# An attention mixture whose code is written out for half tiles of 64 tokens instead of whole tiles of 128

## The chip, the cores and the metric

The kernel runs on one core of a Trainium2 chip, in one launch. The metric is the device time of that launch in microseconds (us); smaller is better. Seven runs of the kernel before gave a median of 4628.34 us (4620.35 to 4635.69).

## The reference, cut to what matters

Four sequences of 1024 tokens with 256 channels go through four layers, each added to its input after a layer norm: a causal attention, a mixture of four attention experts, a second causal attention, and a mixture of 64 small feed-forward experts. The change touches the second layer alone:

```python
logits = x @ router_w + router_b
probs = jax.nn.softmax(logits, axis=-1)
_, top2 = jax.lax.top_k(probs, 2)
for e in range(e_total):                       # 4 experts
    member = (top2 == e).any(-1)
    w_tok = jnp.where(member, probs[..., e], 0.0)
    order = jnp.argsort((~member).astype(jnp.int32), axis=-1, stable=True)
    xg = jnp.take_along_axis(x, order[..., None], axis=1)   # members first
    ...
    q = (xg @ wq[e] + bq[e]).reshape(b, s, h, hd)           # 16 heads of 16
    k, v = ...
    att = jnp.einsum('bqhd,bkhd->bhqk', q, k) * sm_scale
    att = jnp.where(validg[:, None, None, :], att, -1000000000.0)
    att = jax.nn.softmax(att, axis=-1)
    y = jnp.einsum('bhqk,bkhd->bqhd', att, v).reshape(b, s, d)
    y = y @ wo[e] + bo[e]
    out = out.at[bidx, order].add(wg[..., None] * y)
```

Every token belongs to two experts. In each expert a sequence's members attend to each other without a causal mask; tokens that are no members get weight 0, so their rows need not be computed.

Evaluating the reference's first layer and its router on the given inputs gives these numbers of members:

| | expert 0 | expert 1 | expert 2 | expert 3 |
|---|---|---|---|---|
| sequence 0 | 707 | 204 | 346 | 791 |
| sequence 1 | 749 | 189 | 323 | 787 |
| sequence 2 | 705 | 240 | 305 | 798 |
| sequence 3 | 700 | 201 | 333 | 814 |
| largest | 749 | 240 | 346 | 814 |
| tiles of 128 for the largest | 6 | 2 | 3 | 7 |
| half tiles of 64 for the largest | 12 | 4 | 6 | 13 |

## The kernel before

**Routing.** While the first attention runs, `route0` computes each token's rank among the experts, copies the rows of the members of each expert together into an array `xc` in device memory, and counts the tiles that each expert and sequence needs: `more` compares the count with 0, 128, 256, ... (`self.tiles`), and the sum of the comparisons goes into `n_of`.

**The choice of code.** `layer0_ffn` takes for each expert the largest number over the four sequences, loads it into a register and jumps into one of `NT + 1` = 9 copies of the expert's code (`tc.Switch`), written out for 0 to 8 tiles. All four sequences run in the chosen copy, each as one job of `run_attention`. `expert0` builds a job: `prepare` loads and transposes the `n` tiles of rows and makes `kc` (the key mask), `make_qk` projects queries (`pq`, `qa`) and keys (`pk`, `ka`) for a group of four heads, `values` projects the values, and `finish` applies the output matrix.

**Units and steps.** A job has four groups of heads (`g`), and its queries are cut into one half for up to four tiles, or into two (`units_of`): seven tiles become halves of 512 and 384 tokens. A pair of group and half is a unit. Softmax needs each query's largest score first, so a unit has two kinds of step:

- max steps: for one query tile of 128 (`q`), one half of the keys and one pair of heads, two matmuls of 32 contraction rows (L294), whose weights are the 128 queries and whose moving operand is the half's keys; VectorE reduces them to maxima (L309);
- exp steps: for one key tile and one pair of heads, two matmuls (L329) whose weights are 128 keys and whose moving operand is the unit's queries; ScalarE takes the exponential (L340). The negated maximum has been added into a spare row of the queries before (`set_max`: a reduction L365, a transpose of each query tile L372, an addition L376).

`times_v` (L394) multiplies the exponentials with the values: per call four matmuls with weights of 128 rows and 32 columns, each over half of the unit's queries. `divide` copies the sums (L408), transposes them (L412) and divides by the sum of exponentials (L416, L417).

**The order.** `_run_attention` writes TensorE's, VectorE's and ScalarE's orders out by hand in ticks. A tick issues one max step of a unit ahead, one exp step of a unit behind, and one call of `times_v` for exponentials two or three ticks old. `next_max` chooses, of the max steps left in a unit, one that uses the other pair of heads than the tick's exp step and whose width is nearest to it. The four heads of a group lie in rows 0 to 31, 32 to 63, 64 to 95 and 96 to 127, so a tick's four matmuls of L294 and L329 use four different quarters of TensorE's rows.

**Buffers.** PSUM has two score tiles for max steps (`s1`, two banks each), three one-bank tiles for exp steps, transposed maxima and transposed sums (tag `t`), and one bank for the sums `av`.

All matrices are 32-bit floats, and each such matmul appears in the trace as two passes with a weight load each, except for transposes, which take one.

Of the kernel before, what the change touches and what calls it, by code (L numbers as in the profile page):

```python
# [10 lines left out]
F32 = mybir.dt.float32  # L11
# [4 lines left out]
AF = mybir.ActivationFunctionType  # L16
# [5 lines left out]
P = 128  # L22
# [22 lines left out]
class Kernel:  # L45
# [121 lines left out]
        self.n_v += 1  # L167
        return self.v_buf[self.n_v % 2]

    def project(self, w, g, xnT, name, n=NT):  # L170

        nc = self.nc
        pt = self.ps.tile([P, 2, 512], F32, tag="s", name=name)
        for h in range((n + 3) // 4):
            wd = min(512, n * P - h * 512)
            for c in range(2):
                nc.tensor.matmul(  # L177
                    pt[:, h, 0:wd],
                    lhsT=w[:, c, g * P : (g + 1) * P],
                    rhs=xnT[:, c, h * 512 : h * 512 + wd],  # L180
                    start=(c == 0),
                    stop=(c == 1),
                )
        return pt.rearrange("p h t -> p (h t)")[:, 0 : n * P]

    def project_v(self, w, xnT, v, n=NT):
        nc = self.nc
# [44 lines left out]
    def units_of(self, job, causal):  # L232

        n = job["n"]
        first = n if n <= 4 else (n + 1) // 2
        halves = [(0, first * P)] + ([(first * P, (n - first) * P)] if n > first else [])
        units = []
        for g in range(NG):
            for k, (at, w) in enumerate(halves):
                nq = w // P  # L240
                u = dict(job=job, g=g, k=k, q0=at, nq=nq, es={}, last=k == len(halves) - 1)

                parts = halves[: k + 1] if causal else halves
                u["n_half"] = len(parts)
                u["max"] = [
                    (q, half, pair) for q in range(nq) for half in range(len(parts)) for pair in range(2)
                ]
                u["halves"] = parts
                n_kt = (at + w) // P if causal else n

                u["kts"] = [n_kt - 1, n_kt - 2, *range(n_kt - 2)] if causal else list(range(n_kt))
                u["exp"] = [(kt, pair) for kt in u["kts"] for pair in (1, 0)]
                units.append(u)
        return units
# [10 lines left out]
    def next_max(self, u, b, causal):  # L265


        left = u["left"]
        if b is None:
            return left.pop(0)  # L270
        o, (kt, pair) = b
        width = o["nq"] * P - self.exp_from(o, kt, causal)
        best = min(
            left, key=lambda s: (s[2] == pair, abs(self.max_width(u, s, causal) - width))
        )
        left.remove(best)
        return best

    def both(self, a, b, causal, c=None):
# [5 lines left out]
        if a is not None:  # L285
            u, (q, half, pair) = a
            qa, ka = u["qk"]
            q0 = u["q0"] + q * P
            k0 = u["halves"][half][0]
            w = self.max_width(u, (q, half, pair), causal)  # L290
            s = self.ps.tile([P, 2, 512], F32, tag="s", name="s1")
            for jj in range(2):
                r = 32 * (2 * pair + jj)
                nc.tensor.matmul(  # L294
                    s[:, jj, 0:w],
                    lhsT=qa[r : r + 32, q0 : q0 + P],
                    rhs=ka[r : r + 32, k0 : k0 + w],
                    start=True,
                    stop=True,
                )  # L300
            mx = u["mx"][:, q, 2 * pair : 2 * pair + 2, half]

            def maxima(s=s, w=w, diag=causal and half == u["k"]):
                if diag:
                    d = s[:, :, w - P : w]
                    nc.vector.tensor_tensor(  # L306
                        d, d, self.mask.unsqueeze(1).to_broadcast([P, 2, P]), ALU.add
                    )
                nc.vector.tensor_reduce(mx, s[:, :, 0:w], AX.X, ALU.max)  # L309

            reduce.append(maxima)
        for part in (b, c):
# [3 lines left out]
            qa, ka = u["qk"]  # L316
            q0 = self.exp_from(u, kt, causal)
            diag = causal and kt * P >= u["q0"]
            end = u["nq"] * P
            e = self.pp.tile([P, 2, 512], F32, tag="e", name="e")  # L320
            u["es"].setdefault(kt, {})[pair] = e, q0
            both = self.ps.tile([P, 2, 512], F32, tag="s", name="s3") if part is c else None
# [33 lines left out]
                )  # L356
        return reduce, exps

    def set_max(self, u):

        nc = self.nc
        nq = u["nq"]
        self.n_mx += 1
        m = self.mx_buf[self.n_mx % 2]
        nc.vector.tensor_reduce(  # L365
            m[:, 0:nq, :, ROW_MAX], u["mx"][:, 0:nq, :, 0 : u["n_half"]], AX.X, ALU.max, negate=True
        )
        yield
        yield
        pm = self.ps_m.tile([P, 512], F32, tag="t", name="pm")  # L370
        for q in range(nq):
            nc.tensor.transpose(  # L372
                pm[:, q * P : (q + 1) * P], m[:, q].rearrange("p h r -> p (h r)"), self.ident
            )
        part = u["qk"][0][:, u["q0"] : u["q0"] + nq * P]
        nc.vector.tensor_tensor(part, pm[:, 0 : nq * P], part, ALU.add)  # L376
        yield

    def times_v(self, u, kt, half):

        nc = self.nc
        first = kt == u["kts"][0]
        if first and half == 0:
            u["av"] = self.ps_av.tile([P, 512], F32, tag="av", name="av")
        pairs = u["es"][kt] if half == 0 else u["es"].pop(kt)
        v = u["job"]["v"]
        end = u["nq"] * P
        for j in range(4):
            e, q0 = pairs[j // 2]
            mid = (q0 + end) // 2  # L390
            c0, c1 = (q0, mid) if half == 0 else (mid, end)
            c = (4 * u["g"] + j) * VW

            nc.tensor.matmul(  # L394
                u["av"][32 * j : 32 * j + 32, c0:c1],
                lhsT=v[:, kt, c : c + 32],
                rhs=e[:, j % 2, c0 - q0 : c1 - q0],
                start=(first and half == 0),
                stop=(kt == u["kts"][-1]),
                skip_group_check=True,  # L400
            )

    def divide(self, u):
# [1 line left out]
        nc = self.nc  # L405
        g, nq, i0 = u["g"], u["nq"], u["q0"] // P
        avs = self.p2.tile([P, 512], F32, tag="avs", name="avs")
        nc.scalar.copy(avs[:, 0 : nq * P], u["av"][:, 0 : nq * P])  # L408
        yield
        pt = self.ps_m.tile([P, 4, 4, 32], F32, tag="t", name="py")  # L410
        for q in range(nq):
            nc.tensor.transpose(  # L412
                pt[:, q].rearrange("p h r -> p (h r)"), avs[:, q * P : (q + 1) * P], self.ident
            )
        rec = self.p2.tile([P, 4, 4], F32, tag="rec", name="rec")
        nc.vector.reciprocal(rec[:, 0:nq], pt[:, 0:nq, :, HD])  # L416
        nc.vector.tensor_tensor(  # L417
            u["job"]["y"][:, i0 : i0 + nq, 64 * g : 64 * (g + 1)].rearrange(
                "p q (h d) -> p q h d", d=HD
            ),  # L420
            pt[:, 0:nq, :, 0:HD],
            rec[:, 0:nq].unsqueeze(3).to_broadcast([P, nq, 4, HD]),
            ALU.mult,
        )
        yield

    def project_out(self, y, wo, give, n=NT):
# [257 lines left out]
    def ffn_constants(self):  # L685
# [21 lines left out]
        for b in range(B):  # L707
# [11 lines left out]
            self.base, pattern=[[T, E0]], base=0, channel_multiplier=0,  # L719
            allow_small_or_imprecise_dtypes=True,  # L720
        )
        self.tiles = rp.tile([1, NT], F32, tag="tiles", name="tiles")
        nc.gpsimd.iota(
            self.tiles, pattern=[[P, NT]], base=0, channel_multiplier=0,
            allow_small_or_imprecise_dtypes=True,
        )
        self.place = fp.tile([P, T], U16, tag="place", name="place")
# [4 lines left out]
    def route0(self, b):  # L732
# [38 lines left out]
        for i in range(NT):  # L771
# [16 lines left out]
        )  # L788
        cnt = rp.tile([P, E0], F32, tag=f"cnt{b}", name="cnt")
        nc.vector.tensor_copy(cnt, pc[:, nb : nb + E0])  # L790
        more = sm.tile([1, E0, NT], F32, tag="more", name="more")
        nc.vector.tensor_tensor(
            more, cnt[0:1, :].unsqueeze(2).to_broadcast([1, E0, NT]),
            self.tiles.unsqueeze(1).to_broadcast([1, E0, NT]), ALU.is_gt,
        )
        nc.vector.tensor_reduce(self.n_of[:, b, :], more, AX.X, ALU.add)
        at = sm.tile([P, NT, E0], F32, tag="at", name="at")
# [66 lines left out]
    def layer0_ffn(self):  # L864
# [18 lines left out]
        for e in range(E0):  # L883

            ahead = self.new_rows()
            for r in range(0, NT, 2):
# [6 lines left out]
            bias = self.out_bias(self.f1, f"bias{e % 2}", ins["f_bv"][e], ins["f_bo"][e], w["o"])  # L893
            following = load(e + 1) if e + 1 < E0 else None
            count = nc.values_load(
                n_tiles[0:1, e : e + 1], min_val=0, max_val=NT,
                skip_runtime_bounds_check_because="a sum of NT comparisons",
            )
            for n in tc.Switch(count, NT + 1):

                jobs = [self.expert0(b, e, n, w, bias, None if b else ahead) for b in range(B)]
                if e == E0 - 1:
# [7 lines left out]
                            pass  # L910
            w = following

    def expert0(self, b, e, n, w, bias, rows):

        nc = self.nc
        cnt = self.routed[b]["cnt"]

        def prepare(job, rows=rows):
# [34 lines left out]
        def make_qk(job, g):  # L953
            qa = self.qk.tile([P, T], F32, tag="qa", name="qa")
            ka = self.qk.tile([P, T], F32, tag="ka", name="ka")
            job["qk", g] = qa, ka
            pq = self.project(w["q"], g, job["xnT"], "pq", n)
            nc.scalar.activation(  # L958
                qa[:, 0 : n * P], pq, AF.Identity, bias=self.f_bq[:, e, g : g + 1], scale=0.5
            )  # L960
            yield
            pk = self.project(w["k"], g, job["xnT"], "pk", n)
            nc.vector.scalar_tensor_tensor(  # L963
                ka[:, 0 : n * P], pk, self.f_bk[:, e, g : g + 1], job["kc"][:, 0 : n * P],
                ALU.add, ALU.add
# [3 lines left out]
        def give(i, m, po):  # L969
# [7 lines left out]
            )  # L977

        return dict(
            n=n, prepare=prepare, make_qk=make_qk, values=values,  # L980
            finish=lambda job: self.project_out(job["y"], w["o"], give, n),
        )

# [629 lines left out]
```

## Time and profile before

| | |
|---|---|
| median of 7 runs | 4628.34 us |
| the profiled execution's own time | 4634.12 us |
| its span, from the first to the last instruction | 4632.4 us |
| mean granted clock of TensorE | 0.952 |
| TensorE busy with matmuls | 4357.2 us, 94% of the span |
| VectorE busy | 2634.6 us, 57% |
| ScalarE busy | 1909.8 us, 41% |
| GpSimd busy | 626.8 us, 14% |
| expert 0's stage (768 tokens) | about 971 to 1730 us |
| experts 1 and 2 (256 and 384 tokens) | about 1730 to 2167 us |
| expert 3's stage (896 tokens) | about 2168 to 3121 us |

Lines marked L and a number are lines of the kernel. A line of the table of groups names line, engine, operation, the tiles out<-in and their shapes; for matmuls "32*128 32x384" is a stationary operand of 32 rows and 128 columns and a moving operand of 384 columns. PE is TensorE's matmuls, PEld its weight loads, DVE VectorE, ACT ScalarE, POOL GpSimd. Matmul ends are modelled, and a matmul's duration holds the time in which it drains, which the next one can overlap; the distance between starts is what a sequence costs.

### The profile page before, as it was taken

How to read it: one execution, taken by the hardware profiler on the slowest of the kernel's cores; microseconds unless marked ns; L12 is line 12 of the kernel's file. 1: busy time of each engine (PE TensorE's matmuls, PEld its weight loads, DVE VectorE, ACT ScalarE, POOL GpSimd, SP SyncE). 2: the span in 40 equal slices, each digit the busy share in tenths (PEclk: the TensorE clock that was granted, in tenths of full speed). 3: DMA queues.
4: the chain of work that ended last, by engine and by line, in shares of the span. 5: the costliest groups of instructions: out<-in, count | busy, mean ns of one | idle time of the engine just before them, and what ended most of it. 6: DMA issues, size and time to landing. Idle time of an engine off the chain costs nothing. (4 is left out here: it accounts for less than half of the span.)

```text
span 4632.4 us, 88434 instructions
## 1 busy us (share of the span) xinstructions
PE 4357.2 (94%) x38042; PEld 2056.9 (44%) x38042; DVE 2634.6 (57%) x4505; ACT 1909.8 (41%) x4087; POOL 626.8 (14%) x671
## 2 busy tenths in 40 slices
PE   7999999979999999898999999997999899998898
PEld 3444445444444445444343444443444444443556
DVE  5766666646556544453666666655767566474232
ACT  1444444525555553343454555451343333233331
POOL 1002020110000000000001010102111423415243
PEclk8999999979999999999999999998999899897999
DMA  6004000010000000000000000001000111102586
GB/s 217 2 1 134 9 20 4 29 39 8 8 8 8 8 30 25 22 26 26 1 9 27 14 27 1 27 10 32 6 1 28 65 37 49 58 29 88 140 188 170
DMA packets 134455, 188.93 MB, mean 41 GB/s; under 512 B 14816, under 2 KB 116448, under 8 KB 133216
## 3 DMA queue, kind: packets, MB, share of 16 engines
q1 hardware_dynamic: 91584, 99.11, 6.8%
q0 software_dynamic: 27264, 66.18, 5.1%
q10 hardware_dynamic: 15136, 17.20, 1.2%
q8 instruction: 314, 5.14, 0.5%
q14 instruction: 157, 1.29, 0.1%
HBM read 83.36 MB, written 99.09 MB: 39 GB/s over the span
## 5 line engine op out<-in xcount | busy, mean ns | idle before, releaser
L340 ACT ACTIVATE e<-s 128x512 f32<-128x512 f32 (+3 forms) x3428 | 1545.9, 499 | 1855.9 <-PE s L329 1067.8
L309 DVE TENSOR_REDUCE mx<-s 128x2 f32<-128x1024 f32 (+3 forms) x1760 | 1725.0, 981 | 757.0 <-PE s L329 604.3
L329 PE MATMUL s<-qa,ka 32*128 32x384 f32 (+3 forms) x7040 | 1884.7, 558 | 57.0 <-ACT e L340 27.6
L294 PE MATMUL s<-ka,qa 32*128 32x384 f32 (+3 forms) x7040 | 1711.1, 565 | 66.9 <-DVE mx L309 24.7
L394 PE MATMUL av<-e,v 128*32 128x256 f32 (+3 forms) x14080 | 951.0, 346 | 22.8 <-ACT e L346 9.1
L294 PEld LDWEIGHTS s<-ka,qa 32*128 32x128 f32 x7040 | 551.9, 190 | 672.7 <-issue 405.7
L329 PEld LDWEIGHTS s<-qa,ka 32*128 32x128 f32 x7040 | 722.3, 188 | 135.8 <-ACT e L340 64.1
L394 PEld LDWEIGHTS av<-e,v 128*32 128x32 f32 x14080 | 298.8, 111 | 793.8 <-issue 712.3
L306 DVE TENSOR_TENSOR s<-s,mask 128x256 f32<-128x256 f32 x512 | 218.8, 427 | 244.5 <-PE s L294 175.8
L975 POOL DMA_DIRECT2D xc<-os x24 | 18.1, 754 | 2008.1 <-DVE os L971 2008.1
L1270 POOL DMA_INDIRECT xs<-rowsx,dest x192 | 184.8, 963 | 223.1 <-DVE dest L1269 157.0
L353 PEld LDWEIGHTS <-ident_b 128*32 128x32 bf16 x4096 | 62.8, 96 | 245.7 <-issue 232.2
L353 PE MATMUL s<-mask_kq,ident_b 128*32 128x128 bf16 x4096 | 154.8, 232 | 0.0
L177 PE MATMUL pq<-xT,wq 128*128 128x512 f32 (+2 forms) x384 | 148.0, 524 | 2.0 <-ACT xT L942 2.0
L93 POOL TENSOR_SCALAR rows<-x,rstd,shift 128x256 f32<-128x256 f32 x96 | 51.8, 554 | 724.8 <-DVE shift L82 714.8
L445 PE MATMUL po<-wo,yT 128*128 128x256 f32 x544 | 129.5, 390 | 11.5 <-ACT yT L440 11.5
L177 PE MATMUL pk<-xT,wk 128*128 128x512 f32 (+2 forms) x384 | 139.1, 499 | 0.1
L963 DVE SCALAR_TENSOR_TENSOR ka<-pk,bk,kc 128x768 f32<-128x768 f32 (+3 forms) x64 | 52.3, 818 | 151.8 <-PE pk L177 151.8
L1441 POOL DMA_INDIRECT sum<-ye,idx x64 | 99.9, 1561 | 159.5 <-DVE ye L1439 90.5
L376 DVE TENSOR_TENSOR qa<-pm,qa 128x512 f32<-128x512 f32 (+2 forms) x160 | 97.1, 607 | 40.0 <-PE pm L372 37.4
L958 ACT ACTIVATE qa<-pq,bq 128x768 f32<-128x768 f32 (+3 forms) x64 | 47.4, 740 | 173.4 <-PE pq L177 173.4
L445 PEld LDWEIGHTS po<-wo,yT 128*128 128x128 f32 x544 | 101.1, 192 | 36.9 <-ACT yT L440 17.2
(205 smaller groups left out, 3274.5 us busy)
## 6 DMA issues: line engine op xcount, KB each, us to landing
xc<-empty SPq DMA_DIRECT2D x4, 4096.0 KB
gu<-in_e_gu SPq DMA_DIRECT2D x64, 256.0 KB
xs<-empty ACTq DMA_DIRECT2D x16, 642.0 KB
xg<-xs SPq DMA_DIRECT2D x64, 160.5 KB
dn<-in_e_dn SPq DMA_DIRECT2D x64, 128.0 KB
sum<-sum SPq DMA_DIRECT2D x12, 512.0 KB
rows<-xc SPq DMA_DIRECT2D x19, 256.0 KB
xc<-os POOLq DMA_DIRECT2D x8, 512.0 KB
```

The lines of the kernel that those rows point to most:

```text
L177: nc.tensor.matmul(pt[:, h, 0:wd], lhsT=w[:, c, g * P : (g + 1) * P], rhs=xnT[:, c, h * 512 : h * 512 + wd], start=(c == 0), stop=(c == 1),)
L294: nc.tensor.matmul(s[:, jj, 0:w], lhsT=qa[r : r + 32, q0 : q0 + P], rhs=ka[r : r + 32, k0 : k0 + w], start=True, stop=True,)
L306: nc.vector.tensor_tensor(d, d, self.mask.unsqueeze(1).to_broadcast([P, 2, P]), ALU.add)
L309: nc.vector.tensor_reduce(mx, s[:, :, 0:w], AX.X, ALU.max)
L329: nc.tensor.matmul(t[:, 0 : end - q0], lhsT=ka[r : r + 32, kt * P : (kt + 1) * P], rhs=qa[r : r + 32, u["q0"] + q0 : u["q0"] + end], start ...
L340: lambda e=e, t=t, jj=jj, w=end - q0: nc.scalar.activation(e[:, jj, 0:w], t[:, 0:w], AF.Exp)
L353: nc.tensor.matmul(t[j : j + 32, 0:P], lhsT=self.ident_b[:, j : j + 32], rhs=self.mask_kq, start=False, stop=True, skip_group_check=True,)
L376: nc.vector.tensor_tensor(part, pm[:, 0 : nq * P], part, ALU.add)
L394: nc.tensor.matmul(u["av"][32 * j : 32 * j + 32, c0:c1], lhsT=v[:, kt, c : c + 32], rhs=e[:, j % 2, c0 - q0 : c1 - q0], start=(first and h ...
L445: nc.tensor.matmul(po[:, q, :], lhsT=yT[:, q, c, :], rhs=wo[:, c, :], start=(c == 0), stop=(c == 1),)
L1270: d = nc.gpsimd.indirect_dma_start(out=self.xs[int(last)][:, :], out_offset=bass.IndirectOffsetOnAxis(ap=at, axis=0), in_=rows[:, i, :], i ...
L1441: nc.gpsimd.indirect_dma_start(out=of[:, :], out_offset=bass.IndirectOffsetOnAxis(ap=idx[:, 0:1], axis=0), in_=ye, in_offset=None, compute ...
```

## The change

The number that chooses the code counts half tiles of 64: `self.halves` holds 0, 64, 128, ..., 960, and `tc.Switch` has 17 arms instead of 9. From the number of half tiles, `expert0` takes the number of tiles `n`, rounded up, and the exact `width`. Rows, keys (`ka`, `kc`), values and the output still go by whole tiles. Queries end at `width`: in their projection, the exp steps' moving operand, `times_v` and `divide`. The keys of the max steps end there too. A last query tile of 64 has 64 weight columns in its max step and 64 rows in `mx`, `set_max` and `divide`, where operations over all query tiles at once become two, one for the whole tiles and one for the half (`even`). `next_max` compares with the exact width. For the causal layers `width` is `n * P`, and for an even number of half tiles it is so too; then the written-out instructions are those of before.

The diff, cut to its core:

```diff
-    def project(self, w, g, xnT, name, n=NT):
+    def project(self, w, g, xnT, name, width=T):
...
-        for h in range((n + 3) // 4):
-            wd = min(512, n * P - h * 512)
+        for h in range((width + 511) // 512):
+            wd = min(512, width - h * 512)
...
         n = job["n"]
+        width = job.get("width", n * P)
         first = n if n <= 4 else (n + 1) // 2
-        halves = [(0, first * P)] + ([(first * P, (n - first) * P)] if n > first else [])
+        halves = [(0, min(first * P, width))] + ([(first * P, width - first * P)] if n > first else [])
...
-                nq = w // P
-                u = dict(job=job, g=g, k=k, q0=at, nq=nq, es={}, last=k == len(halves) - 1)
+                nq = (w + P - 1) // P
+                u = dict(job=job, g=g, k=k, q0=at, nq=nq, w=w, es={}, last=k == len(halves) - 1)
+                u["wq"] = [min(P, w - q * P) for q in range(nq)]
...
-        width = o["nq"] * P - self.exp_from(o, kt, causal)
+        width = o["w"] - self.exp_from(o, kt, causal)
...
+            wq = u["wq"][q]
...
-                    s[:, jj, 0:w],
-                    lhsT=qa[r : r + 32, q0 : q0 + P],
+                    s[0:wq, jj, 0:w],
+                    lhsT=qa[r : r + 32, q0 : q0 + wq],
                     rhs=ka[r : r + 32, k0 : k0 + w],
...
-                nc.vector.tensor_reduce(mx, s[:, :, 0:w], AX.X, ALU.max)
+                nc.vector.tensor_reduce(mx, s[0:wq, :, 0:w], AX.X, ALU.max)
...
-            end = u["nq"] * P
+            end = u["w"]
...
+    def even(self, u):
+        whole = u["w"] // P
+        return [(0, whole, P)] * (whole > 0) + [(whole, u["nq"], u["wq"][-1])] * (whole < u["nq"])
...
-        nc.vector.tensor_reduce(
-            m[:, 0:nq, :, ROW_MAX], u["mx"][:, 0:nq, :, 0 : u["n_half"]], AX.X, ALU.max, negate=True
-        )
+        for a, z, wq in self.even(u):
+            nc.vector.tensor_reduce(
+                m[0:wq, a:z, :, ROW_MAX], u["mx"][0:wq, a:z, :, 0 : u["n_half"]], AX.X, ALU.max,
+                negate=True,
+            )
...
             nc.tensor.transpose(
-                pm[:, q * P : (q + 1) * P], m[:, q].rearrange("p h r -> p (h r)"), self.ident
+                pm[:, q * P : q * P + wq], m[0:wq, q].rearrange("p h r -> p (h r)"),
+                self.ident[0:wq, 0:wq],
             )
...
             nc.tensor.transpose(
-                pt[:, q].rearrange("p h r -> p (h r)"), avs[:, q * P : (q + 1) * P], self.ident
+                pt[0:wq, q].rearrange("p h r -> p (h r)"), avs[:, q * P : q * P + wq], self.ident
             )
...
-        self.tiles = rp.tile([1, NT], F32, tag="tiles", name="tiles")
+        self.halves = rp.tile([1, 2 * NT], F32, tag="halves", name="halves")
...
-            for n in tc.Switch(count, NT + 1):
+            for n in tc.Switch(count, 2 * NT + 1):
...
-    def expert0(self, b, e, n, w, bias, rows):
+    def expert0(self, b, e, halves, w, bias, rows):
+        n, width = (halves + 1) // 2, halves * P // 2
...
-            pq = self.project(w["q"], g, job["xnT"], "pq", n)
+            pq = self.project(w["q"], g, job["xnT"], "pq", width)
             nc.scalar.activation(
-                qa[:, 0 : n * P], pq, AF.Identity, bias=self.f_bq[:, e, g : g + 1], scale=0.5
+                qa[:, 0:width], pq, AF.Identity, bias=self.f_bq[:, e, g : g + 1], scale=0.5
             )
...
-            pk = self.project(w["k"], g, job["xnT"], "pk", n)
+            pk = self.project(w["k"], g, job["xnT"], "pk", n * P)
...
-            n=n, prepare=prepare, make_qk=make_qk, values=values,
+            n=n, width=width, prepare=prepare, make_qk=make_qk, values=values,
```

`divide`'s reciprocal and product run over `self.even(u)` in the same way as `set_max`'s reduction.

More of the change, by code (lines that the diff above doesn't have):

```diff
@@ L183, in project @@
                 )
-        return pt.rearrange("p h t -> p (h t)")[:, 0 : n * P]
+        return pt.rearrange("p h t -> p (h t)")[:, 0:width]
     def project_v(self, w, xnT, v, n=NT):
@@ L300, in both, with maxima @@
                 )
-            mx = u["mx"][:, q, 2 * pair : 2 * pair + 2, half]
-            def maxima(s=s, w=w, diag=causal and half == u["k"]):
+            mx = u["mx"][0:wq, q, 2 * pair : 2 * pair + 2, half]
+            def maxima(s=s, w=w, wq=wq, diag=causal and half == u["k"]):
                 if diag:
@@ L371, in set_max @@
         for q in range(nq):
+            wq = u["wq"][q]
             nc.tensor.transpose(
-                pm[:, q * P : (q + 1) * P], m[:, q].rearrange("p h r -> p (h r)"), self.ident
-            )
-        part = u["qk"][0][:, u["q0"] : u["q0"] + nq * P]
-        nc.vector.tensor_tensor(part, pm[:, 0 : nq * P], part, ALU.add)
+                pm[:, q * P : q * P + wq], m[0:wq, q].rearrange("p h r -> p (h r)"),
+                self.ident[0:wq, 0:wq],
+            )
+        part = u["qk"][0][:, u["q0"] : u["q0"] + u["w"]]
+        nc.vector.tensor_tensor(part, pm[:, 0 : u["w"]], part, ALU.add)
         yield
@@ L386, in times_v @@
         v = u["job"]["v"]
-        end = u["nq"] * P
+        end = u["w"]
         for j in range(4):
@@ L407, in divide @@
         avs = self.p2.tile([P, 512], F32, tag="avs", name="avs")
-        nc.scalar.copy(avs[:, 0 : nq * P], u["av"][:, 0 : nq * P])
+        nc.scalar.copy(avs[:, 0 : u["w"]], u["av"][:, 0 : u["w"]])
         yield
@@ L411, in divide @@
         for q in range(nq):
+            wq = u["wq"][q]
             nc.tensor.transpose(
-                pt[:, q].rearrange("p h r -> p (h r)"), avs[:, q * P : (q + 1) * P], self.ident
+                pt[0:wq, q].rearrange("p h r -> p (h r)"), avs[:, q * P : q * P + wq], self.ident
             )
         rec = self.p2.tile([P, 4, 4], F32, tag="rec", name="rec")
[L416 to L424, printed above, removed]
+        for a, z, wq in self.even(u):
+            nc.vector.reciprocal(rec[0:wq, a:z], pt[0:wq, a:z, :, HD])
+            nc.vector.tensor_tensor(
+                u["job"]["y"][0:wq, i0 + a : i0 + z, 64 * g : 64 * (g + 1)].rearrange(
+                    "p q (h d) -> p q h d", d=HD
+                ),
+                pt[0:wq, a:z, :, 0:HD],
+                rec[0:wq, a:z].unsqueeze(3).to_broadcast([wq, z - a, 4, HD]),
+                ALU.mult,
+            )
         yield
@@ L721, in ffn_constants @@
         )
-        self.tiles = rp.tile([1, NT], F32, tag="tiles", name="tiles")
+        self.halves = rp.tile([1, 2 * NT], F32, tag="halves", name="halves")
         nc.gpsimd.iota(
-            self.tiles, pattern=[[P, NT]], base=0, channel_multiplier=0,
+            self.halves, pattern=[[P // 2, 2 * NT]], base=0, channel_multiplier=0,
             allow_small_or_imprecise_dtypes=True,
@@ L790, in route0 @@
         nc.vector.tensor_copy(cnt, pc[:, nb : nb + E0])
-        more = sm.tile([1, E0, NT], F32, tag="more", name="more")
+        more = sm.tile([1, E0, 2 * NT], F32, tag="more", name="more")
         nc.vector.tensor_tensor(
-            more, cnt[0:1, :].unsqueeze(2).to_broadcast([1, E0, NT]),
-            self.tiles.unsqueeze(1).to_broadcast([1, E0, NT]), ALU.is_gt,
+            more, cnt[0:1, :].unsqueeze(2).to_broadcast([1, E0, 2 * NT]),
+            self.halves.unsqueeze(1).to_broadcast([1, E0, 2 * NT]), ALU.is_gt,
         )
@@ L895, in layer0_ffn @@
             count = nc.values_load(
-                n_tiles[0:1, e : e + 1], min_val=0, max_val=NT,
-                skip_runtime_bounds_check_because="a sum of NT comparisons",
+                n_tiles[0:1, e : e + 1], min_val=0, max_val=2 * NT,
+                skip_runtime_bounds_check_because="a sum of 2 NT comparisons",
             )
-            for n in tc.Switch(count, NT + 1):
+            for n in tc.Switch(count, 2 * NT + 1):
                 jobs = [self.expert0(b, e, n, w, bias, None if b else ahead) for b in range(B)]
```

## The prediction

> **What bounds the kernel now.** I read the page first, then the sizes of the experts, then the stage that changes, then its order on TensorE.
>
> ```profile
> PE 4357.2 (94%) x38042; PEld 2056.9 (44%) x38042; DVE 2634.6 (57%) x4505; ACT 1909.8 (41%) x4087; POOL 626.8 (14%) x671
> ```
>
> TensorE is busy 94% of the span. The one group that shows each expert's width is the copy of the queries out of PSUM (the view of line L958):
>
> ```profile
> L958 ACT ACTIVATE qa<-pq,bq x64: 473/740/1007, 979.0 to 3028.2; 128x768 f32<-128x768 f32 x16, 128x256 f32<-128x256 f32 x16, 128x384 f32<-128x384 f32 x16, 128x896 f32<-128x896 f32 x16
> ```
>
> So the arms that run are those of 6, 2, 3 and 7 tiles, as the counts 749, 240, 346 and 814 ask for. In half tiles these are 12, 4, 6 and 13. Only 13 is odd: experts 0, 1 and 2 keep their instructions, and expert 3's queries go from 896 to 832, its second half from 384 to 320. The view by stages shows this stage:
>
> ```profile
> core 0: us, PE busy (x) PEld busy (x) DVE busy (x) ACT busy (x) POOL busy (x), PEclk, DMA share, GB/s
> 2168.00:3121.00 953.00, 938.34 (x7950) 385.35 (x7950) 579.16 (x698) 487.28 (x957) 50.39 (x54) 0.98 0.05 15
> ```
>
> TensorE works 938 of 953 us, VectorE 579, ScalarE 487. A microsecond of TensorE is a microsecond of the stage. The timeline of TensorE shows ticks (start, length, line, count of passes):
>
> ```profile
> 2299.55 0.70 PE L294 MATMUL s<-ka,qa 32*128 32x512 f32 x2
> 2299.56 0.70 PE L329 MATMUL s<-qa,ka 32*128 32x512 f32 x2
> 2300.08 0.59 PE L294 MATMUL s<-ka,qa 32*128 32x512 f32 x2
> 2300.10 0.59 PE L329 MATMUL s<-qa,ka 32*128 32x512 f32 x2
> 2300.62 0.64 PE L394 MATMUL av<-e,v 128*32 128x256 f32 x8
> 2301.19 0.70 PE L294 MATMUL s<-ka,qa 32*128 32x512 f32 x2
> ...
> 2305.99 0.59 PE L294 MATMUL s<-ka,qa 32*128 32x384 f32 x2
> 2306.01 0.59 PE L329 MATMUL s<-qa,ka 32*128 32x384 f32 x2
> 2306.42 0.49 PE L294 MATMUL s<-ka,qa 32*128 32x384 f32 x2
> 2306.43 0.49 PE L329 MATMUL s<-qa,ka 32*128 32x384 f32 x2
> 2306.85 0.64 PE L394 MATMUL av<-e,v 128*32 128x256 f32 x8
> 2307.42 0.59 PE L294 MATMUL s<-ka,qa 32*128 32x384 f32 x2
> ```
>
> The reader is to see two things. The max step (L294) and the exp step (L329) start within 0.01 us and run at the same time, in different row quarters: the max step costs nothing beside an exp step of its width. And `times_v` (L394), of another tile shape, starts only when they end. So a tick is a score phase of 1.07 us at 512 (2299.55 to 2300.62) or 0.86 at 384, and a value phase of 0.57 at 256 columns.
>
> **The change part by part.** I grouped the stage's matmul records by tick. The shortest tick is 1.640 us for widths 512/512 with values of 256, 1.534 with values of 192, 1.426 for 384/384 with 256 and 1.319 with 192. So 128 score columns cost 0.214, and 64 value columns 0.106, about 0.83 ns per column and pass. Means lie higher, because in about every second tick the second exp matmul waits for ScalarE to empty a PSUM buffer: 512/512 with 256 1.759 (90 ticks, without one of 6.24), 384/384 with 256 1.485, a max step of 384 beside an exp step of 512 1.735.
>
> *Ticks.* The order can be worked through from the code. Each job and group has 16 + 12 max steps and 14 + 14 exp steps, before and after: 448 of each in the stage, so no tick is saved. Beside each other stand 384/384 in 180 ticks, 512/512 in 184, and the two mixed in 64. Afterwards 320 stands for 384.
>
> *Gain, narrower score phases.* In 180 ticks both operands shrink by 64 columns: 180 x 0.107 = 19.3 us. In the mixed ticks the 512 side sets the phase: nothing. ScalarE's exponential falls from 490 to an estimated 437 ns (between 595 at 512 and 490 at 384 a column is 0.82 ns), so its waits shrink with it, and TensorE stays the bound.
>
> *Gain, values.* Half of the 448 value phases go from 192 to 160 columns: 224 x 0.053 = 11.9 us.
>
> *Gain, query projection.* 64 columns x 2 channel halves x 2 passes x 0.83 ns = 0.21 us, 16 times: 3.4 us. Keys stay.
>
> The gain is 34.6 us.
>
> *Cost, the half query tile.* It has 4 max steps in each of the 16 groups, 64 in all, with 64 weight columns. Worked through the order, 32 of them have 512 keys and 32 have 320, and all 64 stand beside an exp step of 512, whose weights have 128 columns. L394, with 32 weight columns, is recorded as 128*32, so the shape follows the weights, and these steps become 32*64 beside 32*128. Do they still run together? The records have no 64-column load. What they have is 4,056 places where a matmul follows one of another shape: in none does it start more than 0.071 us before the other's modelled end. After one of the same shape it starts earlier by a median of 0.47 us (32*128), 0.32 (128*32) or 0.16 (128*128). All those shapes share cells of the array, so the rows don't prove that 32*64 and 32*128 in different quarters exclude each other. The cost lies between nothing and a score phase of its own. I take the latter, being nearest to 4,056 rows without exception.
>
> The Trainium skill speaks against this change: its page "TensorEngine Tiling (Array Packing)", section "Key Properties", says that to change the tiling mode, and not only the tile, TensorE must drain, and its "Available Configurations" lists 32x64 and 32x128 as two. The 0.071 us agrees for the shapes that the trace has; no row here shows it for 64 columns. By this rule the steps exclude each other and the sum is the +15 us below; without it, it is the -34 of the first rival.
>
> The price: a score phase at 512 is 1.07 us, of which 2 x 512 x 0.83 ns = 0.85 are streaming and 0.22 the exposed first weight load and the drain. For L394 with 32 weight columns the same rest is 0.57 - 0.42 = 0.15. For 64 columns I take 0.18. A phase for 512 keys is then 1.03 us, for 320 keys 0.71. Such a tick does not wait for ScalarE any more, so it lasts the shortest tick plus this phase: 1.64 + 1.03 - 1.759 = 0.91 more than now, 32 times, 29.1 us; and 1.64 + 0.71 - 1.735 = 0.615, 32 times, 19.7 us. Together 48.8.
>
> *Small things.* The half tile's maxima transpose (L372) has 64 rows, another shape: the overlap of 0.163 between transposes falls to 0.07, less half of 0.109 us of streaming, 16 times: 0.6 us. VectorE's L365, L416 and L417 become two each; for three tiles they take 0.18, 0.23 and 0.36 us, so at most 0.77 x 16 = 12.3 us more. VectorE idles 374 us in this stage, and two yields lie behind each; I take nothing, and 12.3 if this cover is gone. Its maxima get shorter. The comparisons in `route0` are wider by 32 numbers, in one partition, beside the first attention. DMAs and their queues are the same.
>
> *The switch.* TensorE stands still 3.95 us at the jump into expert 3 (2167.12 to 2171.07), until "issue". Jumps there are four, before and after. An arm more is not executed: nothing, and if the gap doubled with the arms, 15.8 us.
>
> **Sum.** 48.8 + 0.6 - 34.6 = 14.8 us slower. The profiled execution (4634.1, its span 4632.4) is 5.8 above the median of the runs shown; on that median it makes 4643.
>
> **The rivals.** *The half tile runs beside the exp step after all.* Then the 48.8 us fall away: 4628 - 34 = 4594, faster. For it: the quarters are different, and TensorE does run four matmuls at once. Against it: the 4,056 rows. It decides the sign by itself: with gains of 34.6, the change is slower only if a half tile's tick costs more than 34.6 / 64 = 0.54 us on average.
>
> *The serialised phases cost little more than the gains.* Ticks after a long one may wait less than now. By differences of means (1.759 - 1.485 for 128 columns, 0.137 per 64) the narrower phases bring 5.4 us more, and with L394's rest of 0.15 the phases cost 1.9 less: +7.5, 4636, within the noise.
>
> *Covers gone.* With the switch's 15.8 us the time is 4659, with VectorE's 12.3 it is 4655. For it: cold code does cost 3.95 us. Against it: only one arm is entered, and VectorE has time.
>
> **How the numbers follow.** A measurement of this kernel can tell about 0.2%, 9.3 us, from no change. I give serialised phases 0.75, of which 0.54 end over that and 0.21 within it; the concurrent case 0.20, faster; the lost covers 0.05, slower. The likeliest case's own range is 4636 to 4663: at the top with the rest of 0.22 (2.6 more), without the absorbed waits (32 x 0.119 + 32 x 0.095 = 6.8) and with VectorE's 12.3 half exposed, about 15.5 above the sum, and a few for the scatter of the runs. The whole range reaches down to the concurrent case, 4592, and up to 4663.
>
> **What would show it.** In the profile after: `qa` 128x832 in expert 3 and nothing else new in experts 0 to 2; L294's line split into 32*128 and 32*64; in the timeline, a 32*64 pair that starts 0.7 or 1.0 us ahead of its tick's exp matmuls (if they start within 0.02 us of each other, the first rival holds); half tiles' ticks of 2.67 and 2.35 us; 320/320 ticks of 1.16 at the least; expert 3's stage near 968 us instead of 953, all other stages as they were. The prediction is wrong if a stage outside expert 3 moves by more than a few us, or if the 320/320 ticks stay at 1.32 because something other than TensorE sets them.

## The result and the profile after

The changed kernel takes 4644.16 us in the median of 18 runs, the kernel before 4623.57 in 44 runs beside them: the ratio is 1.0042, with a 95% interval of 1.0033 to 1.0052. On 4623.57 us that is 19.4 us more (15.3 to 24.0). Times differ by some per cent from session to session, on one chip too (the kernel before has medians from 4477 to 4624 us below), so whole times are compared as a ratio to the kernel before in the same session. Stages and ticks are read from the traces.

The page's first line and the queries' copy (in the view of its line, now L975):

```profile
PE 4370.7 (94%) x38042; PEld 2060.1 (44%) x38042; DVE 2608.2 (56%) x4553; ACT 1883.8 (41%) x4087; POOL 627.1 (14%) x671
```

```profile
L975 ACT ACTIVATE qa<-pq,bq x64: 473/740/955, 978.3 to 3033.5; 128x768 f32<-128x768 f32 x16, 128x256 f32<-128x256 f32 x16, 128x384 f32<-128x384 f32 x16, 128x832 f32<-128x832 f32 x16
```

Expert 3's queries end at 832, the other three experts are as they were. TensorE has as many matmuls as before and is busy 13.5 us longer, while VectorE and ScalarE, which got narrower operands, are busy 26 us less each. The view by stages, for expert 3:

```profile
2168.00:3132.00 964.00, 949.31 (x7946) 388.58 (x7945) 551.43 (x745) 459.54 (x955) 50.67 (x54) 0.98 0.05 14
```

VectorE and ScalarE have less work, and TensorE, which sets the time, has more (949 us, 938 before; the window begins 6 us after the stage does). The groups of this stage by shape (line, engine, shapes, count, busy us, mean ns) show which of TensorE's instructions are new:

```profile
L298 PE MATMUL s<-ka,qa 32*128 32x512 f32 x768 | 220.9, 655 | 3.0 <-DVE ka L980 1.5 <-DVE mx L313 1.5
...
L298 PE MATMUL s<-ka,qa 32*128 32x320 f32 x768 | 162.2, 500 | 1.4 <-DVE mx L313 0.7 <-ACT qa L975 0.3 <-ACT v L201 0.2
...
L298 PEld LDWEIGHTS s<-ka,qa 32*128 32x128 f32 x1536 | 118.5, 188 | 134.2 <-issue 98.6 <-DVE mx L313 17.6 <-DVE ka L980 4.5
...
L298 PE MATMUL s<-ka,qa 32*64 32x512 f32 x128 | 34.4, 613 | 0.0
...
L298 PE MATMUL s<-ka,qa 32*64 32x320 f32 x128 | 24.1, 453 | 0.0
...
L298 PEld LDWEIGHTS s<-ka,qa 32*64 32x64 f32 x256 | 12.3, 129 | 21.4 <-issue 12.3 <-DVE mx L313 9.1
```

256 passes, two for each of 128 matmuls, so 64 max steps, carry the shape 32*64. Each single pass is even a little shorter than its neighbour of 128 columns (613 against 655 ns). The price is only seen in the order, in TensorE's timeline of a group of four such ticks:

```profile
2274.69 1.07 PE L298 MATMUL s<-ka,qa 32*64 32x512 f32 x4
2275.70 1.13 PE L333 MATMUL s<-qa,ka 32*128 32x512 f32 x4
2276.75 0.64 PE L407 MATMUL av<-e,v 128*32 128x256 f32 x8
2277.32 1.07 PE L298 MATMUL s<-ka,qa 32*64 32x512 f32 x4
...
2279.95 0.75 PE L298 MATMUL s<-ka,qa 32*64 32x320 f32 x4
2280.64 1.13 PE L333 MATMUL s<-qa,ka 32*128 32x512 f32 x4
2281.70 0.64 PE L407 MATMUL av<-e,v 128*32 128x256 f32 x8
2282.27 0.75 PE L298 MATMUL s<-ka,qa 32*64 32x320 f32 x4
...
2284.58 0.70 PE L298 MATMUL s<-ka,qa 32*128 32x512 f32 x2
2284.59 0.86 PE L333 MATMUL s<-qa,ka 32*128 32x512 f32 x2
```

In the last two lines, a tick of whole tiles, the exp step starts 0.01 us after the max step. With the half tile it starts 1.01 us later (2274.69 to 2275.70), or 0.69 with 320 keys: a score phase of its own. In all 64 places where a 32*128 matmul follows a 32*64 one, the start lies at most 0.071 us before the modelled end of the one before, as at all 4,056 changes of shape in the trace of before. Such a tick lasts 2.63 us with 512 keys and 2.31 with 320.

The stages, in us. An expert's begins with its first transpose of rows and ends where the next begins; the second attention begins with its first projection, the last layer with its first matmul:

| | expert 0 | expert 1 | expert 2 | expert 3 | second attention | last layer |
|---|---|---|---|---|---|---|
| before | 758.3 | 174.2 | 266.1 | 972.7 | 1166.3 | 322.3 |
| after | 757.4 | 167.9 | 265.0 | 989.2 | 1167.8 | 324.9 |

Expert 3 carries +16.5. Expert 1's 6 us are not the change: its code is the same, and the six executions for which I made this table (before, after, and the first four experiments) show 168 to 169 us four times and 174 twice, one of these in an experiment with the change. The difference is TensorE's granted clock, its share of full speed: near the start of this stage it stands at 0.50 for 17.1 us in the two executions with 174 us, and for 3.4 us in the four others. By the letter, the prediction's sign of being wrong (a stage outside expert 3 that moves by more than a few us) has come about, but not through the change.

### The profile page after: what moved, and what is told of

Same layout as the page of the kernel before. It is cut to its first block, busy times and chain, and to the rows that moved or that the text cites. A ratio compares the mean times of both kernels' runs of the same rounds, so it can differ in the third digit from the quotient of the medians.

```text
span 4643.9 us, 88482 instructions
## 1 busy us (share of the span) xinstructions
PE 4370.7 (94%) x38042; PEld 2060.1 (44%) x38042; DVE 2608.2 (56%) x4553; ACT 1883.8 (41%) x4087; POOL 627.1 (14%) x671
## 4 chain that ended last, share of the span: by engine, by line
PE 64%; DVE 6%; issue 5%; DMA 2%; ACT 1%; another core or an unknown queue 1%; POOL 0%; SPq 0%; POOLq 0%; DVEq 0%; ACTq 0%
PE s L298 20%; PE av L407 12%; PE s L333 9%; PE pq L177 3%; PE pa L177 3%; PE pb L177 2%; PE pk L177 2%; DVE mx L313 2%; PE pgu L1309 2%; PE po L460 2%; PE pv L194 2%; PE py L426 1%; PE pm L384 1%; DMA xg<-xs 1%
## 5 line engine op out<-in xcount | busy, mean ns | idle before, releaser
L344 ACT ACTIVATE e<-s 128x512 f32<-128x512 f32 (+4 forms) x3428 | 1523.4, 492 | 1906.7 <-PE s L333 1103.7
L313 DVE TENSOR_REDUCE mx<-s 128x2 f32<-128x768 f32 (+5 forms) x1760 | 1694.6, 963 | 785.9 <-PE s L333 590.7
L333 PE MATMUL s<-qa,ka 32*128 32x384 f32 (+4 forms) x7040 | 1858.1, 553 | 63.0 <-ACT e L344 27.1
L298 PE MATMUL s<-ka,qa 32*128 32x384 f32 (+4 forms) x7040 | 1683.9, 558 | 66.3 <-DVE ka L980 24.1
L177 PE MATMUL pq<-xT,wq 128*128 128x512 f32 (+3 forms) x384 | 143.4, 511 | 2.1 <-ACT xT L959 1.8
L431 DVE RECIPROCAL rec<-py 128x16 f32<-128x16 f32 (+2 forms) x176 | 40.6, 231 | 144.7 <-PE py L426 134.5
L389 DVE TENSOR_TENSOR qa<-pm,qa 128x512 f32<-128x512 f32 (+3 forms) x160 | 96.1, 601 | 40.2 <-PE pm L384 27.5
```

What stands on the lines that cost most here:

```text
L177: nc.tensor.matmul(pt[:, h, 0:wd], lhsT=w[:, c, g * P : (g + 1) * P], rhs=xnT[:, c, h * 512 : h * 512 + wd], start=(c == 0), stop=(c == 1),)
L298: nc.tensor.matmul(s[0:wq, jj, 0:w], lhsT=qa[r : r + 32, q0 : q0 + wq], rhs=ka[r : r + 32, k0 : k0 + w], start=True, stop=True,)
L313: nc.vector.tensor_reduce(mx, s[0:wq, :, 0:w], AX.X, ALU.max)
L333: nc.tensor.matmul(t[:, 0 : end - q0], lhsT=ka[r : r + 32, kt * P : (kt + 1) * P], rhs=qa[r : r + 32, u["q0"] + q0 : u["q0"] + end], start ...
L344: lambda e=e, t=t, jj=jj, w=end - q0: nc.scalar.activation(e[:, jj, 0:w], t[:, 0:w], AF.Exp)
L389: nc.vector.tensor_tensor(part, pm[:, 0 : u["w"]], part, ALU.add)
```

## The experiments

Theory A is that of the prediction: matmuls of the shapes 32*64 and 32*128 exclude each other, and this price exceeds the gain of the narrower operands. Rival B is that a load of 64 columns runs alone by itself, whatever stands beside it. Rival C is that the loss is not on TensorE at all, but in the switch with its 17 arms, or in VectorE's doubled operations.

**The half tile padded to 128 columns** (e1_pad):

```diff
                 nc.tensor.matmul(
-                    s[0:wq, jj, 0:w],
-                    lhsT=qa[r : r + 32, q0 : q0 + wq],
+                    s[:, jj, 0:w],
+                    lhsT=qa[r : r + 32, q0 : q0 + P],
...
-            pq = self.project(w["q"], g, job["xnT"], "pq", width)
+            pq = self.project(w["q"], g, job["xnT"], "pq", n * P)
...
-                qa[:, 0:width], pq, AF.Identity, bias=self.f_bq[:, e, g : g + 1], scale=0.5
+                qa[:, 0 : n * P], pq, AF.Identity, bias=self.f_bq[:, e, g : g + 1], scale=0.5
```

> The changed kernel, but the half query tile's max step loads 128 query columns as before; for that the queries are projected to the whole tile again. Everything else keeps the half tile's width. Theory A (32*64 beside 32*128 excludes each other): the 64 ticks with a half tile fall from 2.63 and 2.31 us to the level of the ticks of before, 1.76 and 1.74, so 46 us of the change go away and 3.4 come back for the projection: 19 - 46 + 3 = 24 us below the kernel before, about 4600. If the loss came from somewhere else (the switch with 17 arms, VectorE's doubled operations), this stays slower than before by some 15 us.

Measured: 0.9965 (0.9954 to 0.9976), so 16 us below the kernel before (11 to 21). The sign is as theory A has it, the size a little short of 24. Expert 3's stage alone lasts 944.0 us, against 967.6 in the next experiment but one, which ran on the same chip with the instructions of before: 23.6 less. What the rest of the run adds back I can't tell from scatter. Rival C falls: the arms and VectorE's doubled operations are still in this kernel, and the loss is gone.

**The same shape on both sides** (e2_same_shape):

```diff
-                nc.tensor.matmul(
-                    t[:, 0 : end - q0],
-                    lhsT=ka[r : r + 32, kt * P : (kt + 1) * P],
-                    rhs=qa[r : r + 32, u["q0"] + q0 : u["q0"] + end],
...
+                for k0 in range(0, P, cut):       # cut: 64 in a half tile's tick
+                    nc.tensor.matmul(
+                        t[k0 : k0 + cut, 0 : end - q0],
+                        lhsT=ka[r : r + 32, kt * P + k0 : kt * P + k0 + cut],
+                        rhs=qa[r : r + 32, u["q0"] + q0 : u["q0"] + end],
...
```

> The changed kernel, but in a tick with a half query tile the exp step's two matmuls of 128 key columns become four of 64, so that all score matmuls of the tick have the shape 32*64. More instructions, same work. Theory A (the exclusion is one of shapes): the max and exp steps start together again, the 64 ticks fall from 2.63 and 2.31 us to about 1.7, and the kernel is some 27 us below the one before, about 4597. Rival B (a load of 64 columns never runs beside another matmul, whatever its shape): the ticks stay at 2.3 to 2.6 us or get longer, since now the exp steps are of that kind too; 19 us or more above the kernel before.

Measured: 0.9943 (0.9927 to 0.9959), 26 us below the kernel before. Its timeline in the first of the four ticks that were shown above:

```profile
2281.12 0.65 PE L299 MATMUL s<-ka,qa 32*64 32x512 f32 x2
2281.14 0.66 PE L335 MATMUL s<-qa,ka 32*64 32x512 f32 x4
2281.60 0.59 PE L299 MATMUL s<-ka,qa 32*64 32x512 f32 x2
2281.62 0.61 PE L335 MATMUL s<-qa,ka 32*64 32x512 f32 x4
2282.15 0.64 PE L409 MATMUL av<-e,v 128*32 128x256 f32 x8
2282.72 0.65 PE L299 MATMUL s<-ka,qa 32*64 32x512 f32 x2
```

The max step's loads are the same 64 columns as in the changed kernel. Nothing but the shape beside them differs, and it has more instructions, not fewer. They start 0.02 us apart again, and this tick lasts 1.60 us; the mean of the half tiles' ticks without other work is 1.76 us with 512 keys and 1.72 with 320, as before the change. Rival B falls; what excludes is the difference of the shapes 32*64 and 32*128.

**The 17 arms alone** (e3_arms):

```diff
-        n, width = (halves + 1) // 2, halves * P // 2
+        n = (halves + 1) // 2
+        width = n * P
```

> Only the counting in half tiles and the switch with 17 arms: each arm computes whole tiles, so that the code that runs is that of the kernel before. Theory A: no difference, within 0.1% of the kernel before. Rival C (more arms cost time at the jumps, or the larger program elsewhere): slower, by 5 us if the part of the measured 19 us that the stage of expert 3 does not hold comes from there, by 16 if the gaps at the four jumps double.

Measured: 1.0007 (0.9993 to 1.0022). No difference that this can tell; the 16 us of doubled gaps are excluded, 5 us are not. TensorE's gaps at the four jumps are 6.12, 3.37, 0.10 and 4.82 us here, 5.62, 4.05, 1.79 and 3.95 before: 14.4 against 15.4 in all.

**The window moved back by 64** (e4_shift):

```diff
-            wq = u["wq"][q]
+            r0, r1 = self.rows_of(u, q)            # 64, 128 for a half tile; 0, 128 else
+            back = q0 - r0
...
-                    s[0:wq, jj, 0:w],
-                    lhsT=qa[r : r + 32, q0 : q0 + wq],
+                    s[0:r1, jj, 0:w],
+                    lhsT=qa[r : r + 32, back : back + r1],
...
-                nc.vector.tensor_reduce(mx, s[0:wq, :, 0:w], AX.X, ALU.max)
+                nc.vector.tensor_reduce(mx, s[r0:r1, :, 0:w], AX.X, ALU.max)
...
```

> The changed kernel, but the half query tile's max step takes a window of 128 query columns that begins 64 earlier: its first 64 result rows are of queries that have their own step, and are not read; the half tile's maxima stand in rows 64 to 127 and are transposed from there. No 64-column load, and all narrower widths kept, the projection's too. Theory A: 19 - 46 = 27 us below the kernel before, about 4596, 3 us faster than the padded version. If something else than the shape makes the loss: slower than before.

Measured: 0.9945 (0.9929 to 0.9960), 25 us below the kernel before, and so a version that beats both the kernel before and the changed one. Expert 3 takes 938.0 us, 29.6 less than with the instructions of before, and 6 less than padded. Its groups of the stage by shape:

```profile
L299 PE MATMUL s<-ka,qa 32*128 32x512 f32 x896 | 257.6, 655 | 3.0 <-DVE ka L988 1.5 <-DVE mx L314 1.5
...
L299 PE MATMUL s<-ka,qa 32*128 32x320 f32 x896 | 186.7, 496 | 1.2 <-DVE mx L314 0.7 <-ACT qa L983 0.3 <-ACT v L201 0.2
```

There is one shape again. The half tile's 64 max steps load twice the columns they need and are free, since they stand beside an exp step: their ticks with 320 keys last 1.733 us in the mean, those with 384 keys before the change 1.735.

**The price by itself** (e5_split64, e6_split32). The kernel before, with whole tiles everywhere, but the last query tile's max steps in expert 3 in pieces:

```diff
-                nc.tensor.matmul(
-                    s[:, jj, 0:w],
-                    lhsT=qa[r : r + 32, q0 : q0 + P],
...
+                cut = P // 2 if not causal and u["job"]["n"] == 7 and u["k"] and q == 2 else P
+                for c0 in range(0, P, cut):
+                    nc.tensor.matmul(
+                        s[c0 : c0 + cut, jj, 0:w],
+                        lhsT=qa[r : r + 32, q0 + c0 : q0 + c0 + cut],
...
```

In the second `cut` is `P // 4`.

> The price by itself: the kernel before (whole tiles everywhere), but in expert 3 the max step of the second half's last query tile loads its 128 query columns as two matmuls of 64 beside each other in the array, instead of one of 128. Same results, same widths, 64 steps of this kind. Theory A: each such tick gets a score phase of its own, 0.99 us for 512 keys and an estimated 0.78 for 384: 32 x (1.64 + 0.99 - 1.76) + 32 x (1.64 + 0.78 - 1.735) = 50 us more than the kernel before, +1.1%. Rival B (a narrow load runs alone, next to one of its own shape too): two phases for each step, some 110 us. If the shape cost nothing: within 0.2%.

> As the split into two of 64, but into four matmuls of 32 columns (shape 32*32). Theory A, in which any shape other than the neighbour's has to wait: the same 50 us, a few more for twice as many instructions (+1.1 to +1.2%). If the exclusion were a matter of 64 columns alone: no loss, or another one.

Measured: 1.0115 (1.0079 to 1.0151) with 64, 1.0107 (1.0082 to 1.0132) with 32: 53 and 49 us on 4611.5, as theory A has it, from 64 split steps that compute the same numbers. Expert 3's stage lasts 1019.2 us in both, 51.6 more than in the arms alone, whose trace has as much of it at a granted clock of 0.50 (39 us in all three), and 46.5 more than in the trace of before (48 us at that clock). The timeline with 64:

```profile
2278.18 1.09 PE L296 MATMUL s<-ka,qa 32*64 32x512 f32 x8
2279.19 1.13 PE L331 MATMUL s<-qa,ka 32*128 32x512 f32 x4
...
2283.47 0.88 PE L296 MATMUL s<-ka,qa 32*64 32x384 f32 x8
2284.27 1.13 PE L331 MATMUL s<-qa,ka 32*128 32x512 f32 x4
```

Eight passes of 64 columns take one phase together, so narrow loads do run beside each other, and rival B falls here too. The exp step waits for that phase, 1.01 us and 0.80 us. The ticks last 2.64 and 2.43 us, with 32 columns the same. So it is no matter of 64 columns alone: beside 32*128, a shape 32*32 waits as 32*64 does. No other shape was tried beside it.

**Everything in one narrow shape** (e7_all64, e8_all32). The same-shape kernel, with `cut` 64 or 32 for every max and exp step of the three attentions:

```diff
-        cut = P
+        cut = P // 2                      # P // 4 in the second
...
-            wq = cut = u["wq"][q]
+            wq = u["wq"][q]
...
+                for c0 in range(0, wq, cut):
+                    nc.tensor.matmul(
+                        s[c0 : c0 + cut, jj, 0:w],
+                        lhsT=qa[r : r + 32, q0 + c0 : q0 + c0 + cut],
...
```

> From the run in which a half tile's tick had four exp matmuls of 64 key columns: its shortest tick was 1.600 us, 0.04 less than one with 128-column loads (1.640), as if half of the first load were exposed no more. Here all score matmuls of all three attentions are split into 64 columns, so that everything beside each other has the shape 32*64 and the half tile fits in by itself. If the 0.04 us hold in all of the some 1,750 ticks: 30 us below the version with the same shape in the half tiles' ticks (27 below the kernel before), so 97 of 100 of the before's time lie a little below it, about -1.9%. If only the short ticks gain, since the others wait for ScalarE: about half, -1.2%. If twice the number of matmuls costs TensorE's queue more than that, or the causal masks' 128*32 pieces cost more: slower than the version it is made from (-0.57%).

> The same with pieces of 32 columns, four times the score matmuls, shape 32*32 throughout. If the exposed first load shrinks with the columns: a further 0.03 us for each short tick, another 0.3 to 0.5%. If issuing 16 score matmuls of two passes in 1.1 us is more than TensorE's queue can do: ticks above 2 us and a clear loss, 10% or more.

Measured: 0.9934 (0.9918 to 0.9949) and 1.0130 (1.0107 to 1.0154). The first is a miss: the hoped-for 1.2 to 1.9% are 0.66%, not to be told from the version it is made from. The shortest ticks did shrink, to 1.600 us at 512/512 and 1.133 at 320/320, but the median of the 512/512 ticks is 1.780 us, against 1.749 in the same-shape kernel (on another chip). What the short ticks gain, the others give back. That these wait for ScalarE fits the trace (the exp steps' loads wait 90.9 us for line L347's exponentials, 61.4 us for L346's in the same-shape kernel), but no run tests it. With 32 columns it is a miss as well: the kernel loses, where a shrinking first load was to bring 0.3 to 0.5% more, though it loses less than the 10% that a queue at its limit was to cost. Many of its matmul records are missing from the trace, so the cause stays open.

## Why the prediction was right

**Where.** Only expert 3 has an odd number of half tiles, and only its stage moved clear of the scatter, by 16.5 us against a forecast of 14.8 (the same instructions give stages 5.1 us apart: 972.7 before, 967.6 in the arms alone). The 320/320 ticks reach 1.159 us at the least, as forecast: TensorE stays the bound there.

**The price.** The choice between nothing and a phase of its own was made by 4,056 changes of shape without an overlap, none of which had cells of the array to spare. That left room for the first rival, and it could not be closed from the trace of before. The 64 starts in the trace after close it, and the same-shape run shows that the difference of shapes is the reason. The size was a little too high: the ticks are 2.63 and 2.31 us, not 2.67 and 2.35. They are 0.99 and 0.67 us longer than the shortest tick of 1.640, so a phase of 64 columns adds 0.14 us to its streaming of 0.85 and 0.53, nearer to L394's 0.15 than to the 0.18 taken. By the same means as in the sum, 32 x (2.631 - 1.759) + 32 x (2.311 - 1.735) = 46.3 us against 48.8.

**The gain.** Free of the price, with the window moved back, the stage is 29.6 us shorter than with whole tiles, where the sum has 34.6 - 0.6 = 34.0. Where nothing disturbs a tick, the terms of the sum come out: the median tick with a query projection falls from 4.524 to 4.151 us, by 0.373, where score phase, values and projection together were to bring 0.107 + 0.053 + 0.21 = 0.37; with a key projection, which stays whole, it falls from 4.817 to 4.657, by 0.160. What is missing lies elsewhere. Eight ticks of the moved version fall into two stretches (2470 to 2477 and 2928 to 2935 us) in which the granted clock stands at 0.50, as it does not in the same ticks of the arms alone; they last 5.2 us longer than the terms make them. Three ticks, each some 20 us after the output step of the sequence before (at 2465, 2692 and 2917 us), last 2.6 us longer than their terms. The remaining ticks and the stage's two ends gain some 3 us more than the sum has. What the three wait for, and whether narrower ticks bring the lower clock with them, is open: the stage has 35 to 54 us at 0.50 in five traces with narrower queries (the 32-column kernel left out), and 39 to 48 in the four with whole tiles.

**The sum.** With the measured ticks it is 46.3 - 34.0 = 12.3 us, where the stage shows 16.5. The trace after has 53.9 us of this stage at a clock of 0.50, the one before 47.7. If TensorE does half its work in that time, the 6.2 us are worth 3.1 at the most, an estimate; the last microsecond stays open. That the sum of 14.8 came within 2 us of the stage is thus partly luck. For the whole run it lies just below the interval of the measured 19.4 us (15.3 to 24.0), and where the rest comes from isn't shown; the interval of the arms alone, from 3 us less to 10 more, leaves room for it. The forecast time of 4643 us is nearer to the measured 4644 than that because it started from a median of 4628 in seven runs, where 44 runs give 4624.

**The Trainium skill's rule**, that TensorE drains when the tiling mode changes ("TensorEngine Tiling (Array Packing)", "Key Properties"), holds here for 32*64 and 32*128 in different quarters of the rows too: 0.071 us of overlap at most in 64 of 64 places. One pair of recorded shapes is different. The half tile's transposes of sums, recorded as 128*64, stand next to 128*128 transposes in 17 places of the trace after, and overlap them by 0.163 us, as 128*128 transposes do each other. Whether these two are different modes the trace does not say, so a new shape in the records is a warning and not yet a price.

**The covers held.** VectorE's doubled operations did not show: its busy time in the stage fell from 579 to 551 us, and the padded and the moved version have them and are faster than before. The gaps at the jumps did not grow: 13.2 us in all after, 15.4 before.

## What to carry to other kernels

Before a tile is cut to its exact size, look at what runs beside it: on TensorE a matmul that shares its shape with its neighbours can be free (128 columns beside 128, or 64 beside 64), and a smaller one of another shape can cost a phase of its own (64 or 32 columns beside 128). If a remainder is narrower than the shape, keep the shape and let a window overlap what is computed already, or cut the neighbour to the same shape. A gain that is spread over many instructions (here 0.11 to 0.16 us in each of 180) and a cost in few (0.9 and 0.6 us in 64) have to be summed before the sign is known.

## What the runs showed of the hardware that was not expected

When all score matmuls of a tick have 64-column loads, the shortest tick is 1.600 us instead of 1.640, and the record of a load lasts 130 to 132 ns instead of 188 to 190. That less of the phase's first load is exposed would explain it, but is not shown by itself. Four matmuls of two passes became eight without any cost in the shortest tick; with sixteen of 32 columns the kernel is 1.3% slower.
